# Gates of the first units moved into the head, gates that stay in SBUF, and a new order of small steps in a scan-and-convolution block

## The chip, the cores and the metric

The kernel runs on one core of one Trainium2 chip. The metric is the device time of one execution in microseconds (us), lower is better. The engines are TensorE (PE, its weight loads PEld), VectorE (DVE), ScalarE (ACT), GpSimd (POOL) and SyncE (SP, which issues the DMAs). Each engine works through its own instructions in the order in which they were written; semaphores make one wait for another.

## The reference

The input x is 4 x 128 x 96 x 96, float32. It is group-normalized (32 groups), read as four sequences of 9216 positions per image (rows, rows backwards, columns, columns backwards), and each sequence goes through this block; the four results are mixed by one more 1x1 product and added to x.

```python
t = grouped1x1(x, in_proj_w, in_proj_b, 4)        # 128 -> 512 channels
u, gate = t[:, :256], t[:, 256:]
u = silu(u)
u = depthwise_conv(u, dw_w)                       # 5 taps along the sequence
s = conv1x1(u, ssm_in_w)                          # 256 -> 32
a = DMIN + (DMAX - DMIN) * sigmoid(conv1x1(u, ssm_delta_w, ssm_delta_b))
bb, cc = tanh(conv1x1(u, ssm_b_w, ...)), tanh(conv1x1(u, ssm_c_w, ...))
h[t] = a[t] * h[t-1] + bb[t] * s[t]               # written there with cumsum and exp
u = u + conv1x1(cc * h + ssm_d * s, ssm_out_w)    # 32 -> 256
u = grouped1x1(u * sigmoid(gate), mix_w, mix_b, 4)
y = conv1x1(u, out_proj_w, out_proj_b)            # 256 -> 128
```

## The kernel before

**Phases, steps, pairs.** There are eight phases: for each of the four images one over columns (`V`) and one over rows (`H`). Both directions of an order are worked on together: a *pair* is two *units*, unit s = 0 walking forwards from one end and s = 1 backwards from the other. A phase has 6 *steps* (`NS`) of 16 lines, and a step has 4 pairs (`R`), one for each residue p of the position modulo 4, in the order `TURN` = 1, 2, 3, 0. So there are 192 pairs of 384 positions per unit, 24 in a phase (`NP`); k = t % 4 is a pair's place in its step. The pairs with p = 0 and p = 3 (k = 2 and k = 3) are `single`: one of their convolution's products covers only an edge.

**What one pair does.** In the loop's turn t, `pair_on(t)` works on three ages of pair at once. For pair t + 4 it makes the front (`front`: input projection on PE, silu on ScalarE into `sil`), though only where the step is `fresh`: in the second half of a phase the two directions meet what the first half has made, so `sil` comes back from DRAM (`load_silu`). A turn that makes a front is called *fronted* (turns of the steps 5, 0 and 1 of a phase); the turns of the steps 2, 3 and 4 are without front. For pair t it makes the convolution: `taps` on VectorE for the second half of the channels (the first tap on ScalarE), `conv` on PE for the first, then either `conv_less` (k = 0, 1: the `less` products on PE and a copy of the result from PSUM into u by ScalarE) or `add_lone` (k = 2, 3: VectorE adds an edge, `lone`, that was written to DRAM by `keep_lone` and comes back by `load_lone`). At the end of the turn `proj` makes the four projections from u, and ScalarE's tanh into `tm` (L802) is the first reader of its result; one such tanh marks each pair. For pair n = t - 6 (`LAG`) it finishes: `under` copies u into the PSUM banks of the output product (ScalarE, L560), `out_of` adds the output product there (PE, L548), `gating` multiplies by 1 + tanh of the gate (VectorE, L664), and a turn later `accumulate` makes the final product (PE, `w_fin`), which ScalarE copies to `ys` and GpSimd adds to `acc`.

**The recurrence.** `scan` runs on VectorE in two parts per step, at k = 0 and k = 1 of the next step. `outputs` on GpSimd multiplies by c (L845), adds d*s (L846, this is z) and copies z (L848), for the pair of five turns ago. `recurrence(t)` issues both; at k = 1 `outputs` needs the scan part that was issued just ahead of it on VectorE.

**Gates.** `gate` makes a unit's gate on PE and a tanh on ScalarE writes it to one of two tiles, `gates`, one turn ahead of its use. It is also stored (`kept`), since the second half of the phase uses the first half's gates backwards (`mirror`); `load_kept` brings them back. Units 0 to 2 of the next phase are made in turns 17 to 19 of a phase, through a tile `shared` of which there is one, and stored as well; `load_gate` brings the inputs of later gates.

**Statistics of the next image.** While a V phase runs, `stats_chunks` collects sums of the next image; in the following H phase `stats_finish`, a generator, is advanced by two pieces in each turn with k = 2 or 3.

**The order** of everything is the order in which these functions issue it. The first eight turns are made by `pair`, whose gates for units 0 and 1 come in turns 6 and 7, and turn 8 makes those of pair 2 as an extra. PSUM has eight banks, and nearly each turn uses all of them: bank numbers are in the code (`PROJ` = 4, 5; `FRONT` = 7, 6, 2, 3; `SSM` and `TAPS` from 0).

Of the kernel before, what the change touches and what calls it, by code (L numbers as in the profile page):

```python
# [47 lines left out]
P = 128  # L48
# [8 lines left out]
R = 4  # L57
# [11 lines left out]
def conv_preact_kernel(  # L69
# [54 lines left out]
    GATE = {True: (6, 4, 5, 7), False: (4, 7, 6, 5)}  # L124

    def plan(with_front):

        return (PROJ, FRONT[:2]) if with_front else (FRONT[:2], PROJ)
# [52 lines left out]
    def stats_finish(b):  # L181

        if b != b0:
            yield
# [7 lines left out]
        if b != b0:  # L197
            yield
# [14 lines left out]
        if b != b0:  # L213
            yield
        inv = sp.tile([P, 2], F32, tag="inv", name=f"inv_{b}")
        if b == b0:
            std = sp.tile([P, 2], F32, tag="err", name="std")
            nc.scalar.activation(std, var, AF.Sqrt)

            nc.scalar.activation(first_table, std[:, 0:1], AF.Silu)  # L220
            nc.vector.reciprocal(inv, std)
        else:
            bits = inv.bitcast(I32)
            nc.vector.tensor_single_scalar(bits, var.bitcast(I32), 1, ALU.logical_shift_right)
            nc.vector.tensor_scalar(bits, bits, -1.0, float(0x5F3759DF), ALU.mult, ALU.add)
            err = sp.tile([P, 2], F32, tag="err", name=f"err_{b}")
            for turn in range(3):
                if turn:
                    yield
                    yield  # L230
                nc.gpsimd.tensor_mul(err, inv, inv)
                nc.gpsimd.tensor_mul(err, err, var)
                nc.gpsimd.tensor_scalar(err, err, -0.5, 1.5, ALU.mult, ALU.add)
                nc.gpsimd.tensor_mul(inv, inv, err)
        yield
        if b != b0:
            yield
# [4 lines left out]

# [3 lines left out]


        pb = bank(free[0])
        product(pb[:, 0:4], wn, gm4)
        if b == b0:  # L250
            for g in range(4):
                for q in range(R):
                    mm(pb[:, 4 + g : 5 + g], q, wn[0:32, 32 * g : 32 * g + 32], mean[0:32, :], True, True)
            nc.vector.tensor_sub(bn, b_in, pb[:, 0:8])
        else:
            nc.vector.tensor_sub(bn[:, 0:4], b_in[:, 0:4], pb[:, 0:4])
            spread = sp.tile([P, 4], F32, tag="spread", name=f"spread_{b}")
# [6 lines left out]
            for q in range(R):  # L264
                mm(pq[:, 0:4], q, id32, spread, True, True)
# [331 lines left out]
    def tile_of(n):  # L597
        return gates[n % 2]
# [851 lines left out]
```

## Time and profile before

| | |
|---|---|
| median of 3 runs | 1783.57 us (1782.19 to 1784.2) |
| the profiled execution's own time | 1788.7 us |
| its span, first to last instruction | 1787.0 us |
| granted TensorE clock, mean | 0.997 |
| PE busy | 1739.9 us, 97% |
| VectorE, ScalarE, GpSimd busy | 1496.9, 1492.7, 1423.3 us |
| DMA traffic | 417.89 MB, mean 234 GB/s |

The profile is of one execution, some 5 us above the median of the timed runs. Rows of a timeline give the start, the length, engine, line, operation and what it writes and reads. Rows of waits give who waited for whom, us in total, how often, and the longest. A row of windows gives each engine's busy time in a stretch, and the granted clock near its end. Names that end a row after `<-` are inferred: the profile names the last semaphore event before the wait ended.

### The profile page before, as it was taken

Reading aid. Unit: us, or ns where it says so; the run is one execution under the profiler, and the core shown is the slowest. Engines: PE = TensorE matmul, PEld = TensorE weight load, DVE = VectorE, ACT = ScalarE, POOL = GpSimd, SP = SyncE. Lnnn points to the kernel's source line nnn. Section 1 sums busy time; section 2 is a strip of 40 time slices with the busy share of each in tenths; the row PEclk is TensorE's granted clock in tenths of the full one; section 3 lists DMA queues with packets and bytes.
Section 4 is the critical chain, followed back from the end, with each engine's and each line's share of the span. In section 5 each row is a group of like instructions: output and inputs, shape, how many; then the busy total and the mean of one; then the engine's idle time right before and its main releaser. Section 6 shows DMA issues by size and latency. Waiting matters only on the chain.

```text
span 1787.0 us, 54377 instructions
## 1 busy us (share of the span) xinstructions
PE 1739.9 (97%) x22618; PEld 661.0 (37%) x22618; DVE 1496.9 (84%) x1526; ACT 1492.7 (84%) x2551; POOL 1423.3 (80%) x1477
## 2 busy tenths in 40 slices
PE   6999999999999999999999999999999999999998
PEld 3334333443334433344333443334433343334433
DVE  6888888887889888888778988888877888888887
ACT  4888888888888888888888888888888888888875
POOL 3578788877878878887777888888787888888886
PEclk9999999999999999999999999999999999999999
DMA  7775975558996688456798688744889749756464
GB/s 238 213 248 193 304 232 166 202 189 278 292 335 233 233 261 243 143 198 230 249 329 301 217 276 262 225 160 163 276 257 316 260 151 311 239 183 198 166 208 176
DMA packets 193814, 417.89 MB, mean 234 GB/s; under 512 B 17312, under 2 KB 154912, under 8 KB 193568
## 3 DMA queue, kind: packets, MB, share of 16 engines
q1 hardware_dynamic: 193424, 414.37, 70.5%
q8 instruction: 179, 2.93, 0.7%
q14 instruction: 67, 0.55, 0.1%
q10 hardware_dynamic: 144, 0.04, 0.0%
HBM read 250.58 MB, written 163.76 MB: 232 GB/s over the span
## 4 chain that ended last, share of the span: by engine, by line
PE 81%; DMA 8%; ACT 4%; DVE 3%; POOL 2%; issue 1%; SPq 1%; DVEq 0%; ACTq 0%; POOLq 0%
PE psum L135 68%; PE psum L548 8%; PE psum L528 5%; DMA kept<-shared 2%; DVE psum L765 1%; DMA x_in<-in_xs 1%; DMA out<-acc 1%; DMA lone<-edge 1%; ACT sil L498 1%; DMA edge<-sil 1%; ACT psum L560 1%; DVE u L664 1%; DMA xs<-in_xr 1%; ACT psum L763 1%; ACT shared L564 0%
## 5 line engine op out<-in xcount | busy, mean ns | idle before, releaser
L765 DVE SCALAR_TENSOR_TENSOR psum<-sil,small,psum 128x768 f32<-128x768 f32 x576 | 589.0, 1023 | 51.7 <-ACT psum L763 26.3
L135 PE MATMUL psum<-u,main 128*32 128x384 f32 x6144 | 538.2, 491 | 13.8 <-ACT shared L564 7.2
L135 PE MATMUL psum<-u,w_fin 128*32 128x384 f32 (+1 forms) x6192 | 543.1, 485 | 1.6 <-ACT ys L872 0.4
L664 DVE SCALAR_TENSOR_TENSOR u<-gate,psum 128x768 f32<-128x768 f32 x376 | 341.8, 950 | 181.2 <-PE psum L548 65.8
L891 POOL TENSOR_TENSOR acc<-ys,acc 128x384 f32<-128x384 f32 x375 | 411.2, 1119 | 21.2 <-ACT ys L874 4.5
L845 POOL TENSOR_TENSOR t<-t,t 64x384 f32<-64x384 f32 (+1 forms) x192 | 235.3, 1225 | 137.8 <-DVE t L839 84.3
L135 PEld LDWEIGHTS psum<-u,w_fin 128*32 128x32 f32 x6192 | 194.5, 110 | 313.0 <-issue 233.9
L135 PEld LDWEIGHTS psum<-u,main 128*32 128x32 f32 x6144 | 181.4, 110 | 342.6 <-issue 219.6
L560 ACT COPY psum<-u 128x768 f32<-128x768 f32 x380 | 298.2, 799 | 9.2 <-DVE u L664 4.4
L135 PE MATMUL psum<-sil,band 128*32 128x384 f32 x3072 | 285.5, 488 | 0.3 <-ACT gate L570 0.3
L846 POOL TENSOR_TENSOR t<-t,t 64x384 f32<-64x384 f32 (+1 forms) x192 | 272.3, 1418 | 15.1
L812 POOL TENSOR_SCALAR t<-tm 64x384 f32<-64x384 f32 x191 | 177.1, 927 | 110.3 <-ACT tm L802 84.0
L763 ACT ACTIVATE psum<-sil,small 128x768 f32<-128x768 f32 x191 | 172.5, 903 | 86.0 <-DVE u L664 83.6
L548 PE MATMUL psum<-t,main 32*128 32x384 f32 x1536 | 209.6, 524 | 4.5 <-ACT psum L560 3.3
L813 POOL TENSOR_TENSOR t<-t,tm 64x384 f32<-64x384 f32 x192 | 196.7, 1025 | 16.8 <-ACT t L805 1.6
L765 DVE SCALAR_TENSOR_TENSOR u<-sil,small,psum 128x768 f32<-128x768 f32 x192 | 194.9, 1015 | 6.9
L498 ACT ACTIVATE sil<-psum,bnorm 128x385 f32<-128x385 f32 x384 | 192.2, 584 | 3.9 <-PE psum L135 1.8
L528 PE MATMUL psum<-x_in,wn 32*128 32x384 f32 x768 | 167.9, 495 | 3.6 <-DVE shift L259 1.4
L135 PEld LDWEIGHTS psum<-sil,band 128*32 128x32 f32 x3072 | 89.8, 108 | 171.3 <-issue 60.6
L874 ACT COPY ys<-psum 128x384 f32<-128x384 f32 x281 | 129.5, 477 | 14.9 <-PE psum L135 11.8
L564 ACT ACTIVATE gate<-psum,bnorm 128x384 f32<-128x384 f32 x148 | 85.8, 581 | 57.1 <-PE psum L528 56.8
L802 ACT ACTIVATE tm<-psum,small 128x384 f32<-128x384 f32 x192 | 111.1, 579 | 11.6 <-PE psum L135 3.4
(105 smaller groups left out, 1512.0 us busy)
## 6 DMA issues: line engine op xcount, KB each, us to landing
sil<-sil SPq DMA_DIRECT2D x128, 770.0 KB, 6.5
gate<-kept SPq DMA_DIRECT2D x113, 768.0 KB, 6.2
kept<-gate SPq DMA_DIRECT2D x75, 768.0 KB, 3.6
lone<-edge SPq DMA_DIRECT2D x46, 770.0 KB, 7.3
x_in<-in_xs SPq DMA_DIRECT2D x194, 96.2 KB, 3.9
edge<-sil SPq DMA_DIRECT2D x96, 192.5 KB, 6.9
out<-acc SPq DMA_DIRECT2D x48, 384.0 KB, 7.9
kept<-shared SPq DMA_DIRECT2D x21, 768.0 KB, 5.2
```

What stands on the lines that cost most here:

```text
L135: nc.tensor.matmul(o[r, : rhs.shape[-1]], lhsT, rhs, start=start, stop=stop, skip_group_check=True)
L498: nc.scalar.activation(sils[step][:, s, j, g, :], bank(bk)[:, : N + 1], AF.Silu, bias=bn[:, 1:2] if j else bn[:, 4 + g : 5 + g],)
L528: nc.tensor.matmul(bank(to)[:, :N], stats[un["b"]][0][r, s, :], x_in[s][r, q, off : off + N], start=True, stop=True)
L548: nc.tensor.matmul(bank(ssm(bi, s) + j)[:, :N], w_so[r, bass.ts(j, P)], z[r, :], start=bi not in seeded, stop=True, skip_group_check=True)
L560: nc.scalar.copy(psum[:, ssm(bi, s) : ssm(bi, s) + 2, :N], us[bi][:, s])
L664: nc.vector.scalar_tensor_tensor(v, g, 1.0, pz, ALU.add, ALU.mult)
L763: nc.scalar.activation(part, src, AF.Copy, scale=w_tap[:, 0:1])
L765: nc.vector.scalar_tensor_tensor(us[i][:, :, 1, :] if k == K - 1 else part, src, w_tap[:, k : k + 1], part, ALU.mult, ALU.add,)
L813: nc.gpsimd.tensor_mul(ta[0:64, p, :], tb[0:64, :], tm[0:64, :])
L845: engine.tensor_mul(ta[0:64, p, r], tb[64:P, r], ta[64:P, p, r])
L846: engine.tensor_add(tb[0:64, r], ta[0:64, p, r], tb[0:64, r])
L891: adder.tensor_add(part, y, part)
```

## The change

The change consists of these parts.

1. The turns 0 to 5 (`pair`) make the gates of units 0 to 5, one unit in a turn; VectorE copies u there and GpSimd scales s. Turns 6 and 7 go through `pair_on` like all later ones. The old code for later turns is gone.
2. In turns without front and with `conv_less`, `under(bi, 0)` is issued ahead of the copies of u.
3. At k = 1, `outputs` is issued behind the two additions of `accumulate`, and no longer ahead of them.
4. `keep_lone` is issued in the front of a step's last part, and `load_lone` always at k = 0.
5. The gates of units 10 and 11 of a phase stay in their tiles for their mirrored use (`stays`), without store and load; `tile_of` turns with the phase. The store of a gate tile is issued behind the loads of the next gates' inputs.
6. `stats_finish` is a table of pieces by turn and place in it, each small product behind the output products, with its small arithmetic on GpSimd; the biases' last part is made by 16 small products and no longer by way of `spread`.
7. `stats_chunks` comes behind the gating in turns with `conv_less`; one `scale_s` moves from turn 19 of a phase to turn 20.

In number of instructions: gate<-kept loads 113 to 98, kept<-gate stores 75 to 58, kept<-shared 21 to 22, lone<-edge 46 to 47; on PE 20 small products more and 16 `less` products fewer; on GpSimd 23 instructions more, on VectorE 16 and on ScalarE 14 fewer.

```diff
@@ stats_finish: pieces by (turn, place)
+        def spreads():
+            nc.vector.tensor_copy(mean, pm[:, 0:1])
+            nc.gpsimd.tensor_sub(dev, mv[:, 0:1], mean)
+            nc.gpsimd.tensor_mul(ex, dev, dev)
+            nc.gpsimd.tensor_add(ex, ex, mv[:, 1:2])
+            nc.gpsimd.tensor_scalar(gm4, gmask, mean, None, ALU.mult)
...
+        return {
+            (0, 0): gather,
+            (1, 1): means,
+            (1, 2): spreads,
+            (2, 1): variances,
+            (2, 2): lambda: nc.vector.tensor_scalar_add(var, pm[:, 0:2], GN_EPS),
+            (3, 0): guess,
+            (4, 0): newton,
+            (5, 0): newton,
+            (6, 0): scale_w,
+            (7, 1): biases,
+            (7, 2): finish,
+        }
@@ after_front
+        if g == R - 1 and fresh(step):
+            keep_lone(step)
@@ gates
     def tile_of(n):
-        return gates[n % 2]
+        return gates[(n + (n + NP // 2) // NP) % 2]
+    def stays(m):
+        return NP // 2 - 3 < m < NP // 2
@@ load_kept
-        if n % NP < 3 and NP <= n < NU // 2:
+        if n % NP < 3 and 1 < n < NU // 2:
             nc.sync.dma_start(tile_of(n), kept[n // NP % 2][n % NP])
-        if n < NU // 2 - R and m is not None:
+        if n < NU // 2 - R and m is not None and not stays(m):
             nc.sync.dma_start(tile_of(n), kept[n // NP % 2][m])
@@ pair, turns 0 to 5
+        if t == R:
+            load_lone(1)
         if t:
             new_u(i)
             taps(i, range(1, K))
             conv(i, banks)
-            conv_less(i, banks)
+            conv_less(i, banks, False)
+            for s in range(2):
+                nc.vector.tensor_copy(us[i][:, s, 0, :], bank(min(banks) + s)[:, :N])
             first_tap(i + 2)
             front(t + R, FRONT if banks == PROJ else (5, 4, 2, 3))
         recurrence(t)
...
         proj(i, banks)
+        n, s = divmod(t, 2)
...
+        for j in range(2):
+            gate(2 * n, s, j, 2 + j)
+        for j in range(2):
+            tanh_one(n, early[0], s, j, 2 + j)
+        load_gate(2 * n + s + UB)
+        if s:
+            nc.sync.dma_start(kept[0][n], early[0])
@@ pair_on
-        if k == 0 and fresh(un["step"]):
-            keep_lone(un["step"])
-        if k == (1 if fresh(un["step"]) else 0):
+        if k == 0:
             load_lone(un["step"])
...
-        recurrence(t)
-        stats_chunks(t)
+        if k < 2:
+            scan(t // R - 1, k)
+        if k != 1:
+            outputs(i - 10)
+        piece(t, 0)
+        if single:
+            stats_chunks(t)
...
+        add_next(w[0])
         if not fronted:
             if not single:
-                conv_less(i, banks)
+                conv_less(i, banks, False)
             under(bi, 0)
+            if not single:
+                copy_u(i, banks)
+        add_next(w[1])
+        if k == 1:
+            outputs(i - 10)
         if fronted:
             if not single:
                 conv_less(i, banks)
+            if t % NP == 20:
+                scale_s(i - 4)
             scale_s(i - 2)
...
         gate_of(0, 1, 5)
+        piece(t, 1)
         for s in range(2):
             gating(bi, s)
...
+        piece(t, 2)
+        if not single:
+            stats_chunks(t)
         first_tap(i + 2)
         if gated is not None:
             tanh_both(gated, to, 0, 6)
-            nc.sync.dma_start(kept[gated // NP % 2][gated % NP], to)
...
+        if gated is not None and not stays(gated % NP):
+            nc.sync.dma_start(kept[gated // NP % 2][gated % NP], to)
...
-        if not fronted:
+        if not fronted and (t % NP != 19 or t + R >= end):
             scale_s(i - 2)
@@ main loop
-        for t in range(LAG + 2):
+        for t in range(LAG):
             pair(t)
-        for t in range(LAG + 2, NU // 2):
+        for t in range(LAG, NU // 2):
             pair_on(t)
```

More of the change, by code (lines that the diff above doesn't have):

```diff
@@ L733, in conv_less, with copy_u @@
                    False, True)
+        if copy:
+            copy_u(i, banks)
+    def copy_u(i, banks):
+        b0 = min(banks)
         if banks == PROJ:
@@ L1030, in pair @@
-        if ending:
-            free[0] = FRONT[0]
-            stats_piece(True)
-        proj(i, PROJ if back else banks, between)
-        if not old and t > 0:
-            scale_s(i - 2)
-        if back:
-            waiting.extend(units[bi : bi + 2])
-        if t >= NU // 2 - 4:
-            load_last(t)
-        if bi > 0 and bi % (NU // B) == 0:
-            send()
+        if t == 2:
+            keep_lone(0)
+        load_chunks(t + 2)
+        proj(i, banks)
+        n, s = divmod(t, 2)
```

298 lines of the change are left out of this document (73 added, 225 removed).

## The prediction

> **What bounds the kernel now.** The page comes first. TensorE (PE) is busy for 97% of the span and no other engine comes near, so time can only come from PE's idle time, or from stretches where PE counts as busy but its columns wait.
>
> ```profile
> span 1787.0 us, 54377 instructions
> PE 1739.9 (97%) x22618; PEld 661.0 (37%) x22618; DVE 1496.9 (84%) x1526; ACT 1492.7 (84%) x2551; POOL 1423.3 (80%) x1477
> ```
>
> Idle is 47 us in all. Busy hides stalls here, though, because a matmul's record spans its pipeline. So I read the beat of the pairs next: the timeline of ScalarE, one tanh into tm per pair, those of pairs 5 and 8, 12 to 14, 22 to 24, 26 and 28.
>
> ```profile
> 69.95 0.59 ACT L802 ACTIVATE tm<-psum,small 128x384 f32<-128x384 f32 x1
> 103.25 0.58 ACT L802 ACTIVATE tm<-psum,small 128x384 f32<-128x384 f32 x1
> ...
> 138.62 0.58 ACT L802 ACTIVATE tm<-psum,small 128x384 f32<-128x384 f32 x1
> 148.04 0.57 ACT L802 ACTIVATE tm<-psum,small 128x384 f32<-128x384 f32 x1
> 156.30 0.58 ACT L802 ACTIVATE tm<-psum,small 128x384 f32<-128x384 f32 x1
> ...
> 230.40 0.58 ACT L802 ACTIVATE tm<-psum,small 128x384 f32<-128x384 f32 x1
> 238.93 0.58 ACT L802 ACTIVATE tm<-psum,small 128x384 f32<-128x384 f32 x1
> 248.26 0.58 ACT L802 ACTIVATE tm<-psum,small 128x384 f32<-128x384 f32 x1
> ...
> 266.04 0.58 ACT L802 ACTIVATE tm<-psum,small 128x384 f32<-128x384 f32 x1
> 285.91 0.58 ACT L802 ACTIVATE tm<-psum,small 128x384 f32<-128x384 f32 x1
> ```
>
> A pair without front takes 9.42 us when it has the `less` products (pair 13, 138.62 to 148.04) and 8.26 us when it has none (pair 14). A fronted pair takes 8.53 (pair 23, the fourth of its step) or 9.33 (pair 24, the first). These are the beats of an undisturbed pair; what is above them is the stage's stall. Pairs 27 and 28 together take 19.87 us for 17.86, and pairs 6 to 8 take 33.3 us.
>
> **Part 1: under(bi, 0) ahead of the copies of u.** This acts in the first and second pair of the steps without front, three steps in each of eight phases. ScalarE, VectorE and PE in pairs 13 and 14, and the wait that counts those pairs:
>
> ```profile
> 141.80 0.48 ACT L874 COPY ys<-psum 128x384 f32<-128x384 f32 x1 [0.17 <-PE psum L135]
> 142.65 0.80 ACT L738 COPY u<-psum 128x768 f32<-128x768 f32 x1 [0.37 <-PE psum L135]
> 143.34 0.81 ACT L560 COPY psum<-u 128x768 f32<-128x768 f32 x1
> 144.07 0.48 ACT L874 COPY ys<-psum 128x384 f32<-128x384 f32 x1
> ...
> 141.11 1.02 DVE L765 SCALAR_TENSOR_TENSOR u<-sil,small,psum 128x768 f32<-128x768 f32 x1
> ...
> 143.90 0.58 PE L528 MATMUL psum<-x_in,wn 32*128 32x384 f32 x1
> 144.29 0.60 PE L548 MATMUL psum<-t,main 32*128 32x384 f32 x3
> 145.79 0.85 PE L135 MATMUL psum<-u,main 128*32 128x384 f32 x8
> ...
> 152.38 0.58 PE L528 MATMUL psum<-x_in,wn 32*128 32x384 f32 x1
> 152.55 0.60 PE L548 MATMUL psum<-t,main 32*128 32x384 f32 x3
> 154.05 1.18 PE L135 MATMUL psum<-u,main 128*32 128x384 f32 x12
> ...
> PEld psum L528 <- ACT u L738: 29.4, 47, 0.6
> ```
>
> The output products (L548) add to the u that under (L560) puts into their banks. In pair 13 that copy ends at 143.34 + 0.81 = 144.15 and the products start at 144.29, 0.39 us after the gate matmul beside which they could run. In pair 14 the lag is 0.17. The whole section from gate to projection is 1.89 us against 1.67. After the change, under needs the last tap (141.11 + 1.02 = 142.13) and stands behind the first ys copy (142.28): it ends by 143.1, ahead of the gate matmul. The copy of u follows until 143.9; the next gate matmul, into bank 7, needs it right behind the first products, and the second ys copy then starts about where it does now. The gain in a pair is between 0.22 (sections as long as pair 14's) and 0.39 (no lag at all); I take 0.28, near the lower end, since the copy of u is now the later one. 47 such pairs are counted in the last row, one of them pair 8, which I cost with the head: 46 x 0.28 = 12.9 us; bounds 0 (the bank of u's copy holds the section as long) and 17.9.
>
> bn_stats now stands behind the gating on VectorE and so delays the next pair's taps where there is a chunk; the copy that waits for the last tap has 0.8 us to spare (143.1 to 143.9), so nothing is charged.
>
> **Part 2: gates that stay, and the store of shared.** In the last pairs of a phase the gates for the next phase go through one tile, `shared`; each tanh waits for the store of the pair before. The wait, the loads' row on the page (count, size, us to landing), one link of the chain, and windows around two stretches of half clock (length, busy time of PE, PEld, DVE, ACT, POOL, clock, DMA share, GB/s):
>
> ```profile
> ACT shared L564 <- DMA kept<-shared: 10.8, 8, 3.1
> ...
> gate<-kept SPq DMA_DIRECT2D x113, 768.0 KB, 6.2
> ...
> 191.90 8.18 DMA kept<-shared
> ...
> 633.30:636.70 3.40, 1.49 (x20) 0.55 (x20) 1.51 (x3) 1.93 (x4) 2.62 (x3) 1.00 0.77 189
> 636.70:640.10 3.40, 3.40 (x36) 0.99 (x44) 3.29 (x4) 1.72 (x4) 0.89 (x1) 0.50 1.01 397
> 920.00:923.40 3.40, 3.40 (x28) 1.01 (x20) 3.26 (x4) 1.49 (x2) 0.31 (x1) 0.50 1.03 390
> ```
>
> The store takes 8.18 us with a load of kept gates and a load of sil issued ahead of it. Units 10 and 11 of a phase now stay in their tiles: 15 of the 113 loads are gone, among them the one ahead of this store, and 17 of the stores. At the 189 to 397 GB/s of the windows a transfer of 768 KB takes 2 to 4 us, so one fewer ahead about covers the longest wait, 3.1. With the stretch at 636.7, which ran 3.4 us at clock 0.50 and so lost 1.7, the part holds 12.5. Moving scale_s out of pair 19 also frees ScalarE there. I take 9, bounds 3 (only the sil load had counted) and 12.5.
>
> A rule of the Trainium skill would leave that 1.7 in place. "TensorE: Matmul & The Clock Gate", Part 1, says that the clock halves only after an idle window of about 3.4 us. In the row ahead of the stretch PE was busy 1.49 of 3.40 us, so this trace does not agree; by the page the stalls of this part and the next cannot have caused the half clock, and 1.7 us of each would stay.
>
> **Part 3: keep_lone in the front of the step's last part.** The edge rows leave one pair earlier, ahead of the output stores, and come back at k = 0 instead of k = 1:
>
> ```profile
> PEld psum L135 <- DVE u L717: 6.0, 3, 2.4
> ...
> 455.47 9.32 DMA out<-acc
> 464.81 8.01 DMA edge<-sil
> 472.89 8.66 DMA lone<-edge
> ```
>
> The edges waited behind four output stores, so add_lone was late three times, at the batch starts. The new order puts them some 9 us ahead. With the stretch at 920.0 (1.7 lost) this holds 7.7 us; I take 5.5, bounds 2 and 7.7. SP now waits for the edges to land before it sends the outputs; behind it stand the outputs and the reload, which have more than a pair.
>
> **Part 4: the statistics in pieces by place.** Pairs 27 and 28 lose 2.0 us: VectorE ran dev, ex and gm ahead of the gating, gm alone 1.25 us. Those go to GpSimd, behind its work. Each small product now stands behind the output products and not ahead of them with a wait:
>
> ```profile
> 274.11 1.25 DVE gm L204
> ...
> 300.95 0.31 PE L135 MATMUL psum<-ex,gmean 128*32 128x1 f32 x16 [0.32 <-ACT ys L874]
> ```
>
> That product cost 0.32 idle and 0.31 of its own; with two more places of this kind that is 1.9, so 3.9 in each of three batches. What stays is 0.31 for this one, half of it for the means, and some 0.6 for the 20 bias products (an estimate from the 16 here, whose shape switches twice), 1.1 together. (3.9 - 1.1) x 3 = 8.4; I take 7.2, bounds 3 and 9.
>
> **Part 5: the head.** Pairs 6 to 8 (33.3 us) become pair_on with their gates done: pair 6 without accumulation at most 8.53, pair 7 8.53, pair 8 9.42 less part 1's 0.28, so 26.2 or less: 7.1 gained. Pairs 0 to 5 each take two gate matmuls and their switches of shape, 0.5 to 0.9 us (the section of four output and four gate matmuls is 1.67): 3 to 5.4 lost. ScalarE's two gate tanhs replace its copies and scale there, and VectorE's two copies fit beside PE. Net 3, bounds -1 (lone_1 late) and 5.
>
> **Part 6: GpSimd adds first at k = 1.** GpSimd's queue in pair 13, and VectorE's scans by group (with one tile, mostly k = 1; with two, k = 0):
>
> ```profile
> 144.05 1.19 POOL L845 TENSOR_TENSOR t<-t,t 64x384 f32<-64x384 f32 x1 [2.69 <-PE psum L135]
> 146.59 0.50 POOL L848 COPY t<-t 64x384 f32<-64x384 f32 x1
> ...
> L839 DVE TENSOR_TENSOR_SCAN t<-t 64x768 f32<-64x768 f32 x56 | 105.1, 1876 | 1.8
> L839 DVE TENSOR_TENSOR_SCAN t<-t,t 64x768 f32<-64x768 f32 x40 | 87.9, 2198 | 1.6 <-POOL t L813 0.3
> ```
>
> GpSimd idles 2.69 us until the scan is done, then c*h, z and its copy take 3.04, to 147.09; z is used at 152.55. With the adds first, the second can start when its ys is there, 144.55, and takes some 1.2; z's copy then ends near 148.9. That leaves 3.6 us, so nothing is charged or gained.
>
> **The sum.** 12.9 + 9 + 5.5 + 7.2 + 3 = 37.6; I take 1.6 off for waits that come late next, the store of pair 19 first: 36. The profiled execution took 1788.7 us (span 1787.0 and 1.7 around it), the median of the three runs is 1783.57, so 1752.7 for the one is 1747.5 for the other.
>
> **The rivals.** (a) The section of part 1 stays as long, because the gate matmul to bank 7 now waits for the copy of u: 23 us gained, 1760.5. For it: that copy ends only as the section starts. Against: the output products, not the gate, were last. 0.14. (b) The queues stay full at the phase ends: parts 2 and 3 bring 3 and 2 for 14.5, so 26.5 and 1757. For it: both half-clock rows show DMA shares above 1. Against: the transfers removed stood directly ahead. 0.12. (c) The half clock at 636.7 and 920.0 has another cause than these stalls and stays: twice 1.7, 3.4 us back, 1751. 0.04. (d) Slower: at k = 1 GpSimd's adds now run beside the scan, on which it waited idle, and hold each other up; z comes after the output products of k = 2. This decides once z slips by more than 3.6 us; to end 4 us above 1783.57, 40 us must be lost in 48 second pairs, 0.83 each, so a slip of 4.4. The rows show 0.32 us between scans beside and without GpSimd's work. "GPSIMD Engine Reference", 8. Key points, of the Trainium skill has the rule: GpSimd shares its SBUF interfaces with VectorE and contends with instructions of two SBUF inputs; the trace agrees in kind. 0.04. (e) The new waits eat the whole gain: 1783. 0.02.
>
> **The numbers.** The forecast has 0.64. Its own bounds reach 1736 (parts 1 and 2 at their upper ends take 8.5 off, the others 3 more); (a) with half of (b) and nothing from part 5 reaches 1767 (23 less 4 and 3). Both and (c) lie inside. A measurement of this kernel tells about 0.2% from no change: faster 0.94, same 0.02, slower 0.04.
>
> **What would show it.** Gate and output matmuls of pair 13 would start within 0.1 us, and its beat be 9.0 to 9.2. Waits of ACT shared on the store under 3 us, of add_lone on its DMA none; clock 0.50 nowhere behind 100 us. Pairs 27 and 28 at 18.2 or less; tm of pair 8 near 100. Wrong would be: a fronted pair, or one with 8.26, grown by 0.1 (10 us in all), or output products that wait for GpSimd.

## The result, and the profile after

The changed kernel took 1772.9 us in the median of five runs (1770.0 to 1778.2), the kernel before 1784.2 beside it: 0.993 of the time, 95% interval 0.9904 to 0.9956. It is 11.3 us faster where 36 were forecast, and its time lies above the range of 1736 to 1767 us. The profiled execution took 1776.2 us with a span of 1774.4, 12.6 us less than the span before. Page of the changed kernel:

```profile
span 1774.4 us, 54440 instructions
PE 1733.1 (98%) x22658; PEld 644.0 (36%) x22658; DVE 1483.2 (84%) x1510; ACT 1488.9 (84%) x2537; POOL 1475.1 (83%) x1500
```

The beat of the pairs is now read where PE starts a pair's projection (timeline of PE; pairs 12, 13, 14, then 26 and 28 of the changed kernel):

```profile
133.19 2.79 PE L130 MATMUL psum<-u,main 128*32 128x384 f32 x32
142.30 2.79 PE L130 MATMUL psum<-u,main 128*32 128x384 f32 x32
150.68 1.80 PE L130 MATMUL psum<-u,main 128*32 128x384 f32 x17
...
260.20 2.12 PE L130 MATMUL psum<-u,main 128*32 128x384 f32 x24
278.03 2.45 PE L130 MATMUL psum<-u,main 128*32 128x384 f32 x26
```

Pair 13 takes 9.11 us for 9.42. Pairs 27 and 28 take 17.83 for 19.87; the tanh into tm, which the prediction used, starts late in pair 28 and would hide that. Two parts of the forecast are seen here as they were worked out.

To see where the rest went I took all 192 starts, subtracted from each pair the undisturbed beat of its kind before the change (9.42 or 8.26 without front, 9.33, 9.26, 8.53, 8.53 with it) and added up the differences by place in the phase (t%24). In us, from pair 9 on (differences below zero outside the first row mostly stand under the others):

| place in the phase | before | changed | what stands there |
|---|---|---|---|
| 36 pairs with the full gain of part 1 | 0 | -11.1 | `less` pairs without other stalls |
| 2, 3 | 7.5 | 0.4 | lone edges, statistics |
| 0, 1, 4, 5 | 4.5 | 10.8 | before: statistics (pairs 28, 76, 124); now: mostly kept gates |
| 8 to 14 | 3.2 | 7.9 | before: half of it statistics; now: half of it additions behind the reload of acc |
| 18 to 20 | 12.4 | 12.3 | tanh into shared behind its store |
| the others | 0.3 | -1.4 | |

Together the change is -9.1, with another -0.5 in differences under 0.05 us a pair that the table leaves out, and the head brings 3.2 (projection of pair 8 at 97.76 for 100.99). The waits of the changed kernel name the same places (us in total, times, longest):

```profile
DVE u L633 <- DMA gate<-kept: 19.2, 9, 3.6
ACT shared L582 <- DMA kept<-shared: 12.9, 7, 3.0
DVE t L813 <- POOL t L787: 8.3, 7, 2.0
POOL acc L865 <- DMA sil<-sil: 2.8, 1, 2.8
```

There is no wait of add_lone on its load any more, but there is a new and longer one: the gating on the load of kept gates. The wait on the store of shared has not fallen at all, 12.9 for 10.8. Both point to SP's queue. First the phase end, where SP issues (timeline):

```profile
179.02 0.35 SPq L424 DMA_DIRECT2D xs<-in_xr  x1
179.46 3.05 SPq L315 DMA_DIRECT2D x_in<-in_xs  x4
182.63 0.51 SPq L1035 DMA_DIRECT2D kept<-shared  x1
```

The chain that ended last runs through this store to the tanh of the next pair:

```profile
182.63 4.64 DMA kept<-shared
...
187.29 0.02 ACTq L582
```

The store of pair 17 goes out at 182.63, 5.46 us behind that pair's projection (177.17), behind the load of a chunk of x and four loads for gates. SP issued nothing from 174.4 to 179.0: the load of the chunk needs a buffer that bn_stats has to release, and bn_stats now stands behind the gating. Before, the store of the same pair left 2.4 us behind the projection, at 183.54 behind 181.16.

Then the edge rows, at t = 23:

```profile
230.22 3.25 SPq L671 DMA_DIRECT2D edge<-sil  x4
233.56 0.65 SPq L493 DMA_DIRECT2D sil<-sil  x1
234.31 2.36 SPq L609 DMA_DIRECT2D gate<-kept  x2
```

Four edge stores and a load of sil stand ahead of two loads of kept gates; the first of these landed at 242.90, 8.6 us after its issue, and the gating waited 1.0 us for it, at other places up to 3.6.

Last, GpSimd at the third reload of a batch (SP, then GpSimd):

```profile
516.74 3.85 SPq L671 DMA_DIRECT2D edge<-sil  x4
520.69 0.82 SPq L607 DMA_DIRECT2D gate<-kept  x1
521.55 3.41 SPq L958 DMA_DIRECT2D acc<-in_xr  x4
...
531.88 4.73 POOL L865 TENSOR_TENSOR acc<-ys,acc 128x384 f32<-128x384 f32 x4 [2.10 <-DMA xs<-in_xr]
```

The reload stands behind the edges too; the additions wait 2.1 us, here and in two other batches 2.8 and 1.2, and GpSimd stays late until the scan of the next step waits for it.

One thing must be known to read the times. In pair 16 `load_kept` writes the gates of unit 9 into `tile_of(12)`, which is the tile that still holds unit 11's; units 14 and 15 have no load. So in the changed kernel units 11, 14 and 15 of a phase take the gates of 9, 9 and 8. The waits show it: in e1 below, the gating of unit 11, whose gates were made in the same tile, waits for a load.

```profile
180.12 1.82 DVE L633 SCALAR_TENSOR_TENSOR u<-gate,psum 128x768 f32<-128x768 f32 x2 [0.92 <-DMA gate<-kept]
```

Two tiles cannot keep units 10 and 11 while 12 and 13 use the gates of 9 and 8, so item 5 in the list of the change does not do what it says. The change as it stands leaves out 16 loads and 16 stores that a kernel with every unit's own gates would make; e9 tells what they weigh.

### The profile page after: what moved, and what is told of

It reads as the page before. It is cut to its first block, busy times and chain, and to the rows that moved or that the text cites. A ratio compares the mean times of both kernels' runs of the same rounds, so it can differ in the third digit from the quotient of the medians.

```text
span 1774.4 us, 54440 instructions
## 1 busy us (share of the span) xinstructions
PE 1733.1 (98%) x22658; PEld 644.0 (36%) x22658; DVE 1483.2 (84%) x1510; ACT 1488.9 (84%) x2537; POOL 1475.1 (83%) x1500
## 4 chain that ended last, share of the span: by engine, by line
PE 83%; DMA 6%; DVE 4%; ACT 3%; POOL 2%; issue 1%; SPq 0%; DVEq 0%; POOLq 0%; ACTq 0%
PE psum L130 71%; PE psum L566 7%; PE psum L546 5%; DMA kept<-shared 2%; DMA gate<-kept 2%; DVE u L633 1%; DVE psum L739 1%; ACT psum L737 1%; POOL acc L865 1%; DMA acc<-in_xr 0%; ACT psum L578 0%; DVE t L813 0%; DMA xs<-in_xr 0%; DVE u L739 0%; ACT shared L582 0%
## 5 line engine op out<-in xcount | busy, mean ns | idle before, releaser
L865 POOL TENSOR_TENSOR acc<-ys,acc 128x384 f32<-128x384 f32 x375 | 438.6, 1191 | 92.6 <-ACT ys L846 41.0
L820 POOL TENSOR_TENSOR t<-t,t 64x384 f32<-64x384 f32 (+1 forms) x192 | 275.3, 1434 | 15.0
L819 POOL TENSOR_TENSOR t<-t,t 64x384 f32<-64x384 f32 (+1 forms) x192 | 245.8, 1280 | 19.9 <-DVE t L813 5.5
L566 PE MATMUL psum<-t,main 32*128 32x384 f32 x1536 | 224.5, 525 | 4.4 <-ACT psum L578 4.3
L546 PE MATMUL psum<-x_in,wn 32*128 32x384 f32 x768 | 161.5, 496 | 0.0
```

What stands on the lines that cost most here:

```text
L546: nc.tensor.matmul(bank(to)[:, :N], stats[un["b"]][0][r, s, :], x_in[s][r, q, off : off + N], start=True, stop=True)
L566: nc.tensor.matmul(bank(ssm(bi, s) + j)[:, :N], w_so[r, bass.ts(j, P)], z[r, :], start=bi not in seeded, stop=True, skip_group_check=True)
L819: engine.tensor_mul(ta[0:64, p, r], tb[64:P, r], ta[64:P, p, r])
L820: engine.tensor_add(tb[0:64, r], ta[0:64, p, r], tb[0:64, r])
L865: adder.tensor_add(part, y, part)
```

## The experiments

Later comparisons ran on chips where the kernel before took 1793 to 1794 us, so kernels are compared by their ratio to the kernel before on the same chip; an interval is 0.001 to 0.003 to each side. The columns of stalls are worked out as in the table above, each from one execution. They scatter: the changed kernel lost 10.8, 7.9 and 12.3 us there in the first trace, 17.9, 5.0 and 9.9 in e5. A single difference of a few us says little.

| kernel | ratio, 95% interval | 0, 1, 4, 5 | 8 to 14 | 18 to 20 |
|---|---|---|---|---|
| changed, again (e5) | 0.9934, 0.9919 to 0.995 | 17.9 | 5.0 | 9.9 |
| e1 store first | 0.9898, 0.9879 to 0.9916 | 18.2 | 6.2 | 4.6 |
| e2 edges behind kept gates | 0.9871, 0.9852 to 0.9889 | 6.2 | 5.5 | 14.4 |
| e3 outputs first | 0.9919, 0.9903 to 0.9934 | 16.3 | 7.2 | 11.5 |
| e4 under back | 0.9976, 0.9965 to 0.9986 | 14.3 | 7.1 | 10.2 |
| e6 = e1 + e2 | 0.9842, 0.9824 to 0.986 | 7.7 | 6.2 | 6.3 |
| e7 = e6 + bn_stats early | 0.9866, 0.9848 to 0.9884 | 8.7 | 6.6 | 3.8 |
| e8 before + under alone | 0.9929, 0.9909 to 0.9949 | 3.1 | 2.7 | 11.2 |
| e9 changed, own gates | 0.994, 0.9918 to 0.9963 | 13.5 | 7.1 | 11.4 |
| e10 = e6, own gates | 0.9875, 0.9852 to 0.9898 | 2.5 | 5.3 | 7.8 |
| e11 = e10, lone as before | 0.9899, 0.9871 to 0.9926 | 1.9 | 4.8 | 8.3 |
| e12 = e10 + acc order | 0.9842, 0.9819 to 0.9865 | 0.5 | 7.1 | 10.1 |
| e13 = e10 + edges behind reload | 0.9832, 0.9807 to 0.9856 | 0.3 | 5.7 | 8.5 |
| e14 = e13 + outputs first | 0.9821, 0.9795 to 0.9847 | 0.3 | 3.0 | 10.9 |
| e15 = e13, gates stay | 0.9824, 0.9797 to 0.9851 | 0.3 | 5.2 | 5.1 |

My theory after the result: SP's order, as the change itself rearranged it, took back what the change gained. The rival: the DMA engines are full at these places, and order does not matter.

**e1: the store of a gate tile right behind its last tanh.**

```diff
             tanh_both(gated, to, 0, 6)
+            if not stays(gated % NP):
+                nc.sync.dma_start(kept[gated // NP % 2][gated % NP], to)
...
-        if gated is not None and not stays(gated % NP):
-            nc.sync.dma_start(kept[gated // NP % 2][gated % NP], to)
```

> One edit to the changed kernel: the store of a finished gate tile is issued right behind its last tanh again, ahead of the loads of x for the gates and of the chunk of statistics. Theory (order on SP's queue): in the V phases the store of shared stands behind the load of a chunk, which waits for bn_stats, which the change put behind the gating; at t = 17 it went out 5.46 us behind the pair's projection and not 2.4. The ACT shared waits fall from 12.9 us to under 6, the pairs 18, 66 and 114 lose under 1 us each for 2.56, 1.97 and 1.85, and the kernel takes 1765 to 1769 us. Rival (the DMA engines are full there, order does not matter): waits stay above 10 us and the time at 1772 to 1774.

Waits of e1:

```profile
ACT shared L582 <- DMA kept<-shared: 5.6, 6, 1.5
DVE u L633 <- DMA gate<-kept: 28.2, 14, 5.0
```

The wait on the store fell from 12.9 (11.7 in e5) to 5.6 us and the stalls of the phase end from 12.3 (9.9) to 4.6. The ratio is 0.0036 lower, 6.5 us of 1793, as expected (4 to 8). The rival is out for this place. The gate loads, untouched here, stayed.

**e2: the edges behind the loads of kept gates.**

```diff
-        if g == R - 1 and fresh(step):
-            keep_lone(step)
...
+            if (t + R) % R == R - 1 and fresh((t + R) // R):
+                keep_lone((t + R) // R)
...
         for e in soon:
             load_kept(e)
         soon.clear()
+        if g == R - 1 and fronted and step * UB < NU:
+            keep_lone(step)
```

> One edit to the changed kernel: the edge rows (keep_lone) leave in the same pair as now, but behind the load of the kept gates that the next pair needs, not ahead of it. Theory (order on SP's queue): the four edge stores ahead of that load make it land 9 to 10 us after its issue, and the gating waits for it; with the order turned the waits of DVE on gate<-kept fall from 19.2 us to under 6, pairs 29, 52, 53, 101, 121, 125 and 149 lose under 0.3 us each for 9.7 in all, and the kernel takes 1762 to 1766 us, with no new wait for lone. Rival (the bytes of that stretch set the landing, whatever their order): the wait turns up at add_lone or at the sil loads, and the time is 1771 to 1775.

Waits of e2:

```profile
ACT shared L580 <- DMA kept<-shared: 10.3, 4, 3.0
DVE u L631 <- DMA gate<-kept: 1.1, 1, 1.1
```

The gating waits for kept gates once, 1.1 us, where it waited 19.2 (27.6 in e5), and no wait for lone appears: 0.0063 lower, 11 us. The bytes are the same; only their order changed. Pair 52, one of the seven that the expectation named, still lost 4.0 us, and pair 100 lost 1.9: there loads of x are late (e12).

**e3: the output products ahead of the additions at k = 1 again.**

```diff
-        if k != 1:
-            outputs(i - 10)
+        outputs(i - 10)
...
-        if k == 1:
-            outputs(i - 10)
```

> One edit to the changed kernel: in the second pair of each step GpSimd runs the output products ahead of the additions again, as in the kernel before. Theory (a queue behind a late reload): three times per execution the additions wait 2.1, 2.8 and 1.2 us for acc to be reloaded and the output products stand behind them; undone, the scans at t%24 = 12 wait for nothing and pairs 61, 109 and 157 lose under 0.4 us each for 1.43, 1.44 and 0.77: 1767 to 1770 us. Rival 1 (the additions beside the scan hold each other up in every second pair, 48 times): the gain is over 8 us, with scans of k = 1 shorter by 0.2 us or more. Rival 2 (additions first brings something in the other 45 pairs): 1773 or more.

The theory fell. Pairs 109 and 157 lost 1.57 and 1.19 us, for 1.44 and 0.77 without the edit; only in the first batch did the reload come in time. GpSimd at the reload of the second batch in e3 (timeline):

```profile
973.20 4.73 POOL L865 TENSOR_TENSOR acc<-ys,acc 128x384 f32<-128x384 f32 x4 [2.46 <-DMA acc<-in_xr]
```

The scans wait for GpSimd longer than in the changed kernel (waits of e3):

```profile
DVE t L813 <- POOL t L787: 11.4, 9, 2.1
```

The additions wait for the reload whichever stands first, and all of GpSimd's work behind them is late. It is the reload that has to come earlier (e13). The time is not told apart from the changed kernel, so rival 1 (a gain over 8 us) is out as well.

**e4 and e8: part 1 alone, taken out and put in by itself.** e4 puts the copy of u ahead of under(bi, 0) in the changed kernel; e8 makes only the opposite edit in the kernel before.

```diff
-                conv_less(i, banks)
+                conv_less(i, banks, False)
             under(bi, 0)
+            if not single:
+                copy_u(i, banks)
```

> One edit to the changed kernel: in pairs without front the copy of u goes ahead of under(bi, 0) again. Theory: 46 pairs return from 9.11 to 9.42 us each, so 14 us are lost: 1786 to 1788 us. Rival (the pairs ran ahead of stalls that ate part of the gain, so that undoing costs less): 1776 to 1781 us.

> The kernel before with one edit: under(bi, 0) ahead of the copy of u in pairs without front, everything else as it was. Theory (the beat of these pairs is set by PE's section and by nothing else): 46 pairs x 0.31 us = 14 us, 0.992 of the time before; with this edit alone the whole change is as fast as its first part, so that the other parts sum to nothing. Rival (the gain runs into the waits at the phase ends): undone from the changed kernel it was worth 0.0046; then 0.9955.

The projections of pairs 12 and 13 in e4 (timeline of PE):

```profile
133.71 2.79 PE L130 MATMUL psum<-u,main 128*32 128x384 f32 x32
143.13 2.79 PE L130 MATMUL psum<-u,main 128*32 128x384 f32 x32
```

And in e8:

```profile
136.42 2.79 PE L135 MATMUL psum<-u,main 128*32 128x384 f32 x32
145.53 2.79 PE L135 MATMUL psum<-u,main 128*32 128x384 f32 x32
```

9.42 us in the one and 9.11 in the other: the 0.31 belongs to this edit. Put in alone it gave 0.9929, as expected, and so all that the whole change gives. Taken out it cost 0.0042 (e4 against e5, on another chip), 7.5 us and not 14, as the rival of e4 has it. The traces do not show the rival's reason: the span of e4 is 13.4 us longer than that of the changed kernel and 12.2 longer than that of e5, and its stalls at other places, 31 us in all, are about theirs (30 and 31). Why the times differ by less stays open. The other parts together were worth nothing measurable.

**e5 to e7: the two orders together.** e6 makes the edits of e1 and e2, e7 puts bn_stats ahead of the gating too:

```diff
         piece(t, 0)
-        if single:
-            stats_chunks(t)
+        stats_chunks(t)
...
-        if not single:
-            stats_chunks(t)
```

> The changed kernel itself, beside the combinations of this call, so that they are compared on one chip. Expected: 0.993 of the time before, as in the first comparison, and the same waits: DVE on gate<-kept about 19 us or more, ACT shared on the store about 13.

> Two of the single edits together: the store of a gate tile right behind its tanh, and the edge rows behind the load of the kept gates. Theory (SP's order holds both transfers up, in different places of the step): the two gains add, 0.0032 and 0.0059 of the time before, to 0.984; ACT shared on the store under 6 us, DVE on gate<-kept under 6. Rival (what one frees the other fills, since the same engines carry all): 0.987 or more, no better than the edge rows alone.

> As the pair of edits, and bn_stats ahead of the gating in every pair, as in the kernel before. Theory: a load of a chunk no longer holds SP for bn_stats, so the loads of x behind it go out up to 4 us earlier and the store too; 0.001 to 0.002 better than without, 0.982 to 0.983. Rival: bn_stats ahead of the gating delays v, and so the gate's section, by up to 0.55 us in each of 66 pairs with a chunk: 0.985 or more.

e5 repeated the first comparison: 0.9934, with waits of 27.6 and 11.7 us. e6 came out at 0.9842: the two gains add, 0.0092 below the changed kernel on the same chip (16 us). e7 is 0.0024 above e6, on the side of its rival, but their intervals overlap, and its profile spans the same (1765.4 and 1765.3); whether the place of bn_stats matters once the store goes ahead stays open.

**e9, e10, e15: every unit its own gates.** `tile_of` is `gates[n % 2]` again and every mirrored unit loads.

```diff
-        return gates[(n + (n + NP // 2) // NP) % 2]
+        return gates[n % 2]
...
-        if n < NU // 2 - R and m is not None and not stays(m):
+        if n < NU // 2 - R and m is not None:
...
-        if gated is not None and not stays(gated % NP):
+        if gated is not None:
```

> The changed kernel with one edit: no gates stay in their tiles; every gate tile is stored and every mirrored unit loads its own, 16 loads and 16 stores of 768 KB more, as in the kernel before. (By its waits, the changed kernel loads the gates of unit 9 of a phase into the tile that holds those of unit 11, ahead of the gating of 11, and has no load for units 14 and 15, so that units 11, 14 and 15 take the gates of 9, 9 and 8; here each takes its own.) If the missing transfers brought what the prediction gave them, 3 to 9 us: 0.995 to 0.998 of the time before, with longer waits of ACT shared on the store than 13 us. Rival (the transfers lay in a stretch with room, only the order counts): 0.9934, as the changed kernel.

> The same edit on the kernel with both orders on SP's queue mended (store behind its tanh, edge rows behind the kept gates): 0.9842 without it. Theory (with the order right, the transfers near the phase ends have room): 0.984 to 0.986, ACT shared on the store under 8 us. Rival (the queue is full there and each transfer of 768 KB delays the next store by 2 to 3 us): 0.988 or more.

> As e13, with the gate tiles handled as in the changed kernel: 16 stores and 16 loads of 768 KB fewer, units 11, 14 and 15 of a phase take the gates of 9, 9 and 8. If the transfers at the phase ends still matter once the order is right: 0.002 to 0.004 below e13. Rival, after the pair of e9 and the changed kernel: the same as e13.

e9 is 0.0006 from the changed kernel: while the store goes out late, the transfers left out bring nothing that shows. With the store first it is otherwise in the traces. The wait of the tanh on the store in e13, which makes the transfers, and in e15, which leaves them out:

```profile
ACT shared L580 <- DMA kept<-shared: 9.2, 7, 3.0
...
ACT shared L580 <- DMA kept<-shared: 5.7, 6, 1.4
```

Four kernels have the store first and leave the transfers out (e1, e6, e7, e15): they lose 3.8 to 6.3 us at the phase end, and the store into `kept` from `shared` lands 4.1 to 4.3 us after its issue in the median. Five have the store first and make the transfers (e10 to e14): 7.8 to 10.9 us, and 5.2 to 5.6 to the landing. So with the order right the transfers weigh some 4 us. As a time that is not resolved: e15 is 0.0008 below e13, and e10 0.0033 above e6, between what was expected of it and the rival, with overlapping intervals in both.

**e11: the edges as before.** They leave at k = 0 and come back at k = 1 in steps with front, on e10, and the calls that sent them earlier go.

```diff
-        if g == R - 1 and fresh(step):
-            keep_lone(step)
...
         if t == R:
+            keep_lone(1)
+        if t == R + 1:
             load_lone(1)
...
-        if k == 0:
+        if k == 0 and fresh(un["step"]):
+            keep_lone(un["step"])
+        if k == (1 if fresh(un["step"]) else 0):
             load_lone(un["step"])
```

> As e10, but the edge rows leave at k = 0 and come back at k = 1 of a step with front, as in the kernel before. Theory (the earlier edges are worth the 5.5 us of the prediction once they stand behind the kept gates): waits of add_lone on its load return at the batch starts, 6 to 8 us, and the time is 0.003 above e10. Rival (the move brings nothing even when placed well): the same as e10.

```profile
DVE u L681 <- DMA lone<-edge: 11.0, 4, 4.6
```

The waits return, 11.0 us for the 6 to 8 expected; the stalls at t%24 = 2 and 3 grow from 0.4 to 12.8 us and the span from 1764.5 to 1770.7. The ratio rises by 0.0024; with intervals of 0.0025 the time alone would not tell. Pairs 61, 109 and 157 have no stall here, and the additions no wait for acc: with the edges at k = 0 the reload stands ahead of them. That was the hint for e13.

**e12 and e13: the reload of acc.** In e12 the first reload of a batch goes out four pairs later, since in e6 and the changed kernel SP was so full that loads of x for the front came late. Chain of the changed kernel at pair 52:

```profile
472.77 7.35 DMA xs<-in_xr
...
480.13 6.20 DMA x_in<-in_xs
...
486.47 6.16 PE psum L130 x90
```

The load of x for the front goes out when a chunk lands that was issued long before, and PE waits for it. e12 also runs GpSimd's output products first at t%48 = 9; e13 does not, but sends the edges behind the reload there (the two remarks are not in the code).

```diff
-        if len(reload) == 4 and (k == 1 or late):
-            for b, r in reload:
+        if len(reload) >= 4 and (late or t % (NP * 2) == 6 or k == 1 and t % (NP * 2) != 1):
+            for b, r in reload[:4]:
                 nc.sync.dma_start(accf[:, r], xr[b, :, r])
-            reload.clear()
+            del reload[:4]
+        if edges_due and late:  # e13 only
+            keep_lone(step)
...
-        if k != 1:
+        first = k != 1 or t % (NP * 2) == 9  # e12 only
+        if first:
             outputs(i - 10)
```

> As e10 with two more orders: in the three pairs (t%48 = 9) whose additions wait for the reload of acc, GpSimd runs the output products first; and the first reload of a batch goes out four pairs later, with the second one pair behind it, so that the loads of x for the front do not stand behind it. Theory: pairs 61, 109 and 157 lose under 0.3 us for about 1.1 each, and 52 and 100 under 1 us for 5.7 and 1.8; together 0.003 to 0.005 below e10. Rival (what the reload leaves free the out stores and kept gates fill): waits turn up one or two pairs later and the time is that of e10.

> As e10 (both orders on SP's queue mended, every mirrored unit loads its gates), with the first reload of a batch four pairs later as in e12, without e12's change on GpSimd, and one order more: in the pair of a batch's last reload the four edge stores go out behind the reload of acc, not ahead of it. Theory (the prediction's sentence that outputs and reload have more than a pair is false: the edges ahead of the reload make it land 1.6 to 2.1 us after GpSimd could add, and GpSimd stays late for four pairs): no wait of POOL on acc<-in_xr, pairs 61, 109 and 157 lose under 0.4 us each for 0.97, 1.15 and 1.44 of e12, 0.002 below e12: 0.982. Rival (GpSimd is late there because the additions stand ahead of the outputs at k = 1): these pairs stay above 0.9 and the time at 0.984.

In e12 pairs 52 and 100 lose nothing, but 61, 109 and 157 lose 0.97, 1.15 and 1.44: half of its theory fell as in e3. Its time is 0.0033 below e10, as expected, with overlapping intervals. In e13 SP and GpSimd show:

```profile
517.17 2.84 SPq L958 DMA_DIRECT2D acc<-in_xr  x4
520.06 2.35 SPq L666 DMA_DIRECT2D edge<-sil  x4
...
529.66 4.77 POOL L860 TENSOR_TENSOR acc<-ys,acc 128x384 f32<-128x384 f32 x4
```

The additions wait for nothing, and the three pairs lose under 0.25 us each. The rival, GpSimd's own order, is out for these pairs. The time, 0.9832, is 0.001 from e12, less than the runs resolve, and pairs 58 and 106 now lose 1.34 each. There a scan runs beside two of GpSimd's additions, and both take longer (VectorE, then GpSimd):

```profile
535.73 3.60 DVE L808 TENSOR_TENSOR_SCAN t<-t 64x768 f32<-64x768 f32 x1
...
536.52 3.83 POOL L860 TENSOR_TENSOR acc<-ys,acc 128x384 f32<-128x384 f32 x2
```

The median scan of this kind takes 1.815 us in this trace, and two additions take 2.40 at other places. e11 and e15, whose reload is in time as well, have such scans at the same two places, of 3.57 to 3.73 us.

**e14: outputs first, with the reload in time.** The edit of e3 on e13.

> As e13, with the output products ahead of the additions at k = 1 everywhere, as in the kernel before. With the reload in time this measures that part of the change by itself. If the new order brings nothing and costs nothing, as the prediction had it: the same as e13 within 0.001. If the additions beside the scan cost something: 0.002 or more below e13. If they keep GpSimd ahead and so help: above e13.

0.9821 against 0.9832, the same within the runs. Pairs 58 and 106 lose nothing here, so GpSimd's new order costs about 2.7 us in the trace of e13, by the scans held up beside the additions, and brings nothing; as a time it is not shown. e13, e14 and e15 are not told apart. e14 is the version to keep: 1761.0 us in the median beside 1793.9, 0.9821, with the parts of the change that pay, four orders on SP's queue mended (store, edges behind kept gates, first reload, edges behind the last reload) and every unit's own gates.

## Why the prediction was right and wrong

**Part 1** was right in mechanism and size: 12.9 forecast, 0.31 a pair for the 0.28 taken; alone it gave 0.9929 (e8), 12.7 us of 1793, give or take 3.6. In pair 13 under ends at 139.93, the copy of u at 140.66, and the first gate matmul and output product start within 0.01 us of each other (timelines of ScalarE and PE):

```profile
139.13 0.80 ACT L578 COPY psum<-u 128x768 f32<-128x768 f32 x1
139.87 0.79 ACT L712 COPY u<-psum 128x768 f32<-128x768 f32 x1
...
140.72 0.58 PE L546 MATMUL psum<-x_in,wn 32*128 32x384 f32 x1
140.73 0.60 PE L566 MATMUL psum<-t,main 32*128 32x384 f32 x3
```

**Part 5** was right: 3 forecast, 3.2 found, and the half clock near 94 us is gone. Pairs 6 to 8 take 27.1 us for 33.6, and 27.1 to 27.5 in every trace with this head. What pairs 1 to 5 lose in exchange differs: 3.6 us here, up to 6.7 in e2 and e13, where a stretch of half clock stands at 65 us. **Part 4** was right too: in the first batch pairs 27, 28 and 30 lost 2.55 us, and pairs 38 and 39, where the product by way of `spread` stood, another 0.95; now pairs 25, 26, 31, 38 and 39 lose about 1.0 together. That is 2.5 us a batch and some 7.5 in all for 7.2. These two parts were read from the traces and not tried apart.

**Part 2** failed, 9 forecast and 0.1 found (2.5 in e5). The step that failed is "one fewer ahead about covers the longest wait": it counted the transfers that were gone from in front of the store, and not those that the change puts there. The description of the change names the store behind the loads for gates, but the working of the prediction never went along SP's queue; in part 1 it even noted that bn_stats moves behind the gating, weighed it against the taps alone, and missed the load that waits for bn_stats on SP. e1 mends the order and takes 5 to 8 us off the phase end. It takes both: with the store late the place loses 9.9 to 14.4 us whether the transfers are made (e9) or not (changed, e2 to e5); with the store first and the transfers made, 7.8 to 12.4 (before, e8, e10 to e14); with the store first and without them, 3.8 to 6.3, which is 6 to 9 us less than before. So with the store left where it was the part would have brought most of its 9, the transfers themselves some 4 of it; the change itself broke that condition. And as the units are ordered, two tiles do not let every unit take its own gates and leave the transfers out.

**Part 3** was right in what it took away (the stalls of pairs 50, 98, 99 and 146, 6.0 us by the starts, are gone; 5.5 forecast) and wrong in "behind it stand the outputs and the reload, which have more than a pair". Two loads of kept gates stand there as well, which have less: 9.4 of the 10.8 us of new stalls at t%24 = 0, 1, 4 and 5 (the other 1.4, pairs 52 and 100, are loads of x that stand behind the first reload; e12). And the last reload of a batch has no pair to spare, since GpSimd adds into acc at once: pairs 61, 109 and 157 lose 3.6 us of the 7.9 at 8 to 14. e2 and e13 turn these two orders and the waits go.

**Part 6** said that nothing need be charged. Nothing measurable was found in the time (e3, e14), though not for its reason alone: the outputs queued behind additions that waited, and e13 shows two pairs of 1.34 us, 2.7 in all, in which the additions and the scan hold each other up; e14, without that order, has neither.

With those terms the sum closes roughly: 36, less the 9 of part 2, less the 10.8 at t%24 = 0, 1, 4 and 5, less the 4.7 more at 8 to 14, is 11.5; the medians gave 11.3. That it comes so near is luck, since in e5 the same kernel loses 17.9 and 5.0 us at these places. With the orders mended the change brings 0.0168 in e13 and 0.0179 in e14, 30 and 32 us on that chip. That is near 36, but these kernels hold a move that the change never had (the first reload four pairs later) and make the transfers of part 2, so it does not confirm each size.

Of the rivals, (a) fell, since the section did become shorter: in pair 13 the projection starts 1.58 us behind the first gate matmul (140.72 to 142.30), 1.89 before. (e), new waits that eat the whole gain, given 0.02, is nearest in time and in kind: new waits and one that stayed took two thirds of the gain. It named no cause. (b) put the loss on full queues; e1 and e2 move the same bytes in another order, and the waits fall to 5.6 and 1.1 us. What is left at the phase end when every unit loads its own gates, 8 to 11 us with the store first, may still be fullness; no run settles that. (c), half clock with another cause, was not put to the test, since the stalls stayed and half clock stands behind stalls again (last section); e15, with the fewest of them, was granted a mean clock of 1.000, the kernel before 0.997. (d) fell as it was priced, 40 us: in the mean the scans kept their durations (1894 ns for 1876, 2207 for 2198). Its hold-up is real, though, in the two pairs of e13. What no rival named is that a step moved earlier on a queue makes those behind it late.

## What to carry to other kernels

Where a step moves on a queue that also carries loads, write down the queue as it will stand and give each entry its deadline; moving a transfer up is free only if everything between its new and its old place has time, and an issue that waits for a buffer holds all behind it. Test a change of several parts with its surest part alone (e8): if that gives the whole gain, the rest may be cancelling and not absent. Test an edit again once the fault that hid it is mended: the transfers left out seemed worthless in e9 and not in e15. And see which stall took the gain by the place in the loop at which the beat is longer, rather than by busy shares, which stayed at 97 to 98% here.

## What the runs showed of the hardware

TensorE ran at half clock for 3.4 us behind stretches in which it was far from idle (windows of the changed kernel: length, PE, PEld, DVE, ACT, POOL, granted clock, DMA share, GB/s):

```profile
617.30:620.70 3.40, 1.70 (x16) 0.93 (x16) 2.82 (x5) 1.01 (x3) 3.18 (x4) 1.00 0.97 296
620.70:624.10 3.40, 3.32 (x24) 1.10 (x28) 2.03 (x2) 2.52 (x5) 1.47 (x2) 0.51 1.01 365
1112.30:1115.70 3.40, 2.21 (x44) 0.40 (x38) 2.61 (x3) 1.73 (x3) 0.95 (x2) 1.00 1.06 327
1115.70:1119.10 3.40, 3.40 (x29) 1.14 (x28) 3.29 (x4) 3.32 (x7) 1.73 (x2) 0.50 0.98 361
```

PE was busy for 1.70 and 2.21 of 3.40 us, and the next 3.4 us were granted half. A stall of 2 us can so cost 1.7 more, an estimate from 3.4 us at half the clock. It need not: PE was busy for 1.87 us from 566.20 to 569.60, and the next 3.4 us had the full clock.

Transfers of the same 768 KB landed at very different times: the two loads of kept gates behind the edge stores at t = 23 took 8.6 and 9.6 us, while the median of all 98 is 6.9. And in crowded stretches SP issued the next transfer in the moment that the one eight places ahead landed. In the changed kernel 51 of 1043 issues begin within 0.06 us of such a landing, at no other distance more than 15. SP in e6 (timeline):

```profile
464.42 3.58 SPq L960 DMA_DIRECT2D acc<-in_xr  x3
470.10 0.33 SPq L424 DMA_DIRECT2D xs<-in_xr  x1
470.52 0.38 SPq L607 DMA_DIRECT2D gate<-kept  x1
472.19 1.88 SPq L297 DMA_DIRECT2D x_in<-in_xs  x2
474.46 0.53 SPq L491 DMA_DIRECT2D sil<-sil  x1
475.41 0.35 SPq L424 DMA_DIRECT2D xs<-in_xr  x1
```

The chunk in the last row is the eighth behind the reload of acc at 464.42, which landed at 475.39.

A scan on VectorE that ran beside two additions on GpSimd took up to 3.73 us (e15), where the median of its kind is 1.815.
